# A Mamba layer and a mixture of experts on one core: long expert blocks of two sizes, and the seldom needed blocks behind four branches

## The chip, the cores and the metric

The kernel runs on one core of one Trainium2 chip. The metric is device time in microseconds (us); the time before is the median of three runs. Engines are named as in the profile: PE is the matrix engine (PEld its weight loads), DVE the vector engine, ACT the scalar engine, POOL the engine that issues indirect DMAs, SP the engine that issues plain DMAs. A "q" after a name (PEldq, DVEq) is that engine's instruction sequencer.

## The reference

The input is 4096 tokens of 256 numbers. A Mamba layer is added to it and normalised; every token of the result then goes through one of eight experts, and that is added and normalised again. All is float32. The experts are what the change touches:

```python
logits = xf @ Wr.T + br
expert_idx = jnp.argmax(logits, axis=-1)                 # one of 8 for each token
h = relu(einsum('td,efd->etf', xf, W1) + b1[:, None, :])  # 256 -> 1024
y = einsum('etf,efd->etd', h, W2) + b2[:, None, :]        # 1024 -> 256
x = layernorm(x + y[expert_idx, arange(T)])
```

With the inputs that are given, the reference's own arithmetic sends 495, 560, 487, 548, 514, 589, 514 and 389 tokens to the eight experts. In blocks of 128 that leaves 111, 48, 103, 36, 2, 77, 2 and 5 tokens over, and needs 37 blocks.

## The kernel before

The tokens go through Mamba in eight tiles of 512 (project, gauge, scan, gate, project_out). After each tile, choose, rank and place write each token's number into a list that is ordered by expert. The experts then work on blocks of up to 128 tokens of one expert: block b gathers its rows of x1 by an indirect DMA (L461), gathers its expert's weights into one of three buffers, b % 3 (L478), computes, and scatters its rows to the output by another indirect DMA (L589). Which expert and which rows a block has is known on the chip alone, so the number of blocks that the program holds is fixed: 32 that always run (SURE) and 7 more, of 39 in the worst case, that run only when they are needed.

A table tells each block its expert and its rows. Tables for the first 17 blocks are made early, when 3, 5 and 6 tiles are known; the last one (blocks_of, table, lookup) makes blocks 17 to 38 by a chain of small DVE instructions at 291 to 300 us, while blocks 8 and 9 run.

**Long blocks.** Five of the 32 blocks (LONG: 17, 20, 23, 26 and 29) are longer: they take 64 further rows of their expert, so that an expert with up to 64 tokens over needs no block for them. Given the counts above, five experts have 64 or fewer over, and 37 - 5 = 32 blocks are needed. A long block multiplies 192 columns at a time instead of 128 in its first layer (hidden, L526). In its second layer (close) the first 128 rows are done as in any block (pe, L551) and the further rows apart (pf, L562): their 64 columns take half of TensorE's columns, so two of the eight partial products run side by side, into two halves of one PSUM bank, and finish adds the two halves (L584).

**Order of a block.** The blocks function is a generator that yields after each quarter of a block: hidden(b, 0), hidden(b, 1), close(b, 0), close(b, 1). The transposes of the next block's rows (turn, L500 and L502) are put between hidden(b, 1) and close(b, 0). ACT evicts the first half of the hidden layer (L535), DVE the second (L537). After close, finish adds the residual (L573, L575) and normalises: DVE L252, L254 and L256, a square root on ACT (L257), DVE L258 and L259. PE's order is the order of the program; that of the other engines is made by the framework, which keeps what is inside a branch together and in its place. TensorE's results live in eight PSUM banks that one pool hands out in turn: three with the tag mm for hidden (two for an ordinary block, four for a long one), three with the tag o for pe and pf, two with the tag tr for the transposes.

**The branch.** Ahead of block 30 (BRANCH), seldom() gathers the rows of all seven blocks and opens one If on the number of blocks needed (held, read into a register of each engine while block 27 runs); all seven blocks stand in it, their weights loaded by SP. When it is not taken, each engine runs a short other side, which waits for the engine's own work and adds to its semaphore what the seven blocks would have added, and then jumps over the seven blocks. Block 30 is not turned ahead of the branch (`b + 1 not in (BRANCH, SURE)`), but after it.

Of the kernel before, what the change touches and what calls it, by code (L numbers as in the profile page):

```python
# [37 lines left out]
F32 = mybir.dt.float32  # L38
# [9 lines left out]
P = 128  # L48
# [25 lines left out]

EXTRA, MORE = 5, 64
LONG = {EARLY[6] + SLOTS * n: n for n in range(EXTRA)}
assert EXTRA <= RUN


BRANCH = SURE - 2  # L80
EPS = 1e-5
# [17 lines left out]
def mamba_moe(  # L99
# [179 lines left out]
    def table(b0, nb, columns, rows, early):  # L279
# [24 lines left out]
        if longer:  # L304

            low = small("low", [NE], I32)
            nc.vector.tensor_scalar(low, pn[:, 0:NE], float(MORE - 1), None, ALU.add)
            nc.vector.tensor_scalar(low, low, -P, None, ALU.bitwise_and)
            more = small("more", [NE])
            nc.vector.tensor_tensor(more, up, low, ALU.subtract)  # L310
            nth = small("nth", [NE])
            nc.vector.tensor_tensor(nth, low, taken, ALU.is_gt)
            nc.vector.tensor_tensor(more, more, nth, ALU.mult)

            nc.vector.tensor_tensor_scan(nth, ones8, more, 0.0, ALU.mult, ALU.add)
            nc.vector.scalar_tensor_tensor(
                more, nth, float(longer * P), more, ALU.is_le, ALU.mult
            )
            nc.vector.tensor_tensor(nth, nth, more, ALU.subtract)
            base = small("base", [1])  # L320
            nc.vector.tensor_reduce(base, more, AX.X, ALU.add)
            nc.vector.scalar_tensor_tensor(whole, more, -2.0, whole, ALU.mult, ALU.add)

            key = small("key", [NE])
            nc.vector.tensor_scalar(key, more, 0.0, float(OFF), ALU.is_equal, ALU.mult)
            nc.vector.tensor_tensor(key, key, nth, ALU.add)
            mine = small("mine", [longer, NE])
            nc.vector.tensor_tensor(mine, wide(key, longer), number(longer), ALU.is_equal)
            whose = small("whose", [longer, NE])
            nc.vector.tensor_tensor(whose, mine, wide(expertno, longer), ALU.mult)  # L330
            expert_of = small("expert_of", [longer])
            nc.vector.tensor_reduce(expert_of, whose, AX.X, ALU.add)
            nc.vector.tensor_scalar(key, low, -float(P + OFF), None, ALU.add)
            nc.vector.tensor_tensor(key, key, nth, ALU.subtract)
            nc.vector.tensor_tensor(mine, mine, wide(key, longer), ALU.mult)
            row_of = small("row_of", [longer])
            nc.vector.tensor_reduce(row_of, mine, AX.X, ALU.add)
        ends = small("ends", [NE])
        nc.vector.tensor_tensor_scan(ends, ones8, whole, 0.0, ALU.mult, ALU.add)
        if longer:  # L340
            nc.vector.tensor_scalar(ends, ends, base, None, ALU.add)
        starts = small("starts", [NE])
        nc.vector.tensor_tensor(starts, ends, whole, ALU.subtract)
        if not early:
            total = const.tile([1, 1], I32, name="total")
            nc.vector.tensor_copy(total, ends[0:1, NE - 1 : NE])
            held.append(total)
        shift = small("shift", [NE])
        nc.vector.scalar_tensor_tensor(shift, taken, -float(OFF), starts, ALU.add, ALU.subtract)


# [8 lines left out]
        if longer:  # L360
            nc.vector.tensor_tensor(row[:, 0:longer], row[:, 0:longer], row_of, ALU.add)
            nc.vector.scalar_tensor_tensor(
                row[:, nb:], row_of, float(P), blockoff[:, 0:longer], ALU.add, ALU.add
            )
# [10 lines left out]
        if not early:  # L375

            nc.vector.tensor_scalar(
                spare, eb[0:1, SURE - b0 : NSB - b0], float((NE - 1) * P), None, ALU.min
            )


            same = small("same", [nb])
            nc.vector.tensor_tensor(same[:, 1:nb], eb[:, 1:nb], eb[:, 0 : nb - 1], ALU.is_equal)
            nc.vector.memset(same[:, 0:nb:RUN], 0.0)
            nc.vector.scalar_tensor_tensor(eb, same, float(NE * P), eb, ALU.mult, ALU.add)
        widx = const.tile([P, nb], I32, name=f"widx{b0}")
# [10 lines left out]
        def lookup():  # L397

            pi = bank("tr", f"pi{b0}", 2)
            n = nb + longer  # L400
            for h in range(LH):
                nc.tensor.matmul(
                    pi[:, 0:n], lhsT=lists[:, h * P : (h + 1) * P], rhs=pick[:, h, :],
                    start=(h == 0), stop=(h == LH - 1),
                )
            codes = small("codes", [n])
            nc.scalar.copy(codes, pi[:, 0:n])
            half = small("half", [n])
            nc.vector.tensor_scalar(half, codes, 0.0, -float(T + 1), ALU.is_gt, ALU.mult)
            tidx = const.tile([P, n], I32, name=f"tidx{b0}")  # L410
            nc.vector.scalar_tensor_tensor(tidx, codes, float(T), half, ALU.add, ALU.add)
            for b in range(nb):
                index[b0 + b] = rows, tidx[:, order(b0, b)]
            for b, x in LONG.items() if longer else ():
                further[b] = tidx[0:MORE, nb + x : nb + x + 1]

# [39 lines left out]

    xgf, openf, yf, ends_, wide_ = {}, {}, {}, {}, {}
    current = 0
# [7 lines left out]
    def prefetch(b):  # L466
        for n in range(b, min(b + AHEAD, SURE - 1) + 1):
            if n in index and n not in xgs:
                xgs[n] = m3.tile([P, D], F32, tag="xg", name=f"xg{n}", bufs=4)
                gather(xgs[n], *index[n])  # L470
                if n in LONG:
                    ends_[n] = a2.tile([P, CC, KC - 1 + TB], F32, tag="xc", name=f"long{n}")
                    ends_[n] = ends_[n].rearrange("p c t -> p (c t)")
                    xgf[n] = ends_[n][0:MORE, 0:D]
                    gather(xgf[n], index[n][0], further[n])
# [7 lines left out]

    def rows_of(b):
        return P + MORE if b in LONG else P

    def buffer(b):
# [4 lines left out]
        return wide_[b]  # L492

    def turn(b):

        n = rows_of(b)
        px = bank("tr", f"pg{b}", 2)
        for dc in range(DC):
            at = slice(dc * P, (dc + 1) * P)
            nc.tensor.transpose(px[:, dc * n : dc * n + P], xgs[b][:, at], ident)  # L500
            if b in LONG:
                nc.tensor.transpose(  # L502
                    px[:, dc * n + P : (dc + 1) * n], xgf[b][:, at], ident[0:MORE, 0:MORE]
                )
        if b in LONG or b >= SURE:
            turned[b] = buffer(b)[:, FC * n : (FC + DC) * n]
        else:
            turned[b] = m2.tile([P, DC * P], F32, tag="xgT", name=f"xgT{b}")
        nc.vector.tensor_copy(turned[b], px[:, 0 : DC * n])

    def hidden(b, half):
        we, xgT, w = wes[b], turned[b], rows_of(b)
        if half == 0:
# [27 lines left out]
    def close(b, half):  # L541
# [15 lines left out]
        if b in LONG:  # L557

            openf[b] = bank("o", f"pf{b}")
            for fc in range(FC):  # L560
                g = fc % 2 * MORE
                nc.tensor.matmul(  # L562
                    openf[b][g : g + MORE, 0:D], lhsT=hT[:, fc, P:], rhs=out_weights(fc),
                    start=(fc < 2), stop=(fc >= FC - 2), tile_position=(0, g),
                )
        finish(b)

    def finish(b):
# [10 lines left out]
        if b in LONG:  # L579
            xs, r, yf[b] = (ends_[b][0:MORE, n * D : (n + 1) * D] for n in (1, 2, 3))  # L580
            nc.vector.tensor_tensor(xs, xgf[b], we[0:MORE, OC : OC + D], ALU.add)
            for g in range(2):
                part_sum = openf[b][g * MORE : (g + 1) * MORE, 0:D]
                nc.vector.tensor_tensor(r, part_sum, r if g else xs, ALU.add)  # L584
            layernorm(m2, r, yf[b], f"f{b}")
# [10 lines left out]

    def seldom():

        rows = a3.tile([P, CC, TB], F32, tag="cv", name="rows").rearrange("p c t -> p (c t)")
        for b in range(SURE, NSB):  # L600
            xgs[b] = ys[b] = rows[:, (b - SURE) * D : (b - SURE + 1) * D]
            gather(xgs[b], *index[b])
        with tc.If(held[1] > (SURE - EARLY[6]) * P, preferred_fallthrough_block=False):
            for b in range(SURE, NSB):
                wes[b] = held_weights[(BRANCH - 1) % SLOTS]
                row = nc.values_load(
# [10 lines left out]
    def blocks():  # L617

        nonlocal current
        for b in range(SURE):  # L620
            current = b
            if b == BRANCH:
                seldom()
            prefetch(b)

            if 0 < b:
                scatter(b - 1)
            if b == BRANCH:
                for n in range(SURE, NSB):
                    scatter(n)  # L630
            if b not in turned:
# [4 lines left out]
            yield  # L636
            if b + 1 in xgs and b + 1 not in (BRANCH, SURE):
                turn(b + 1)
# [432 lines left out]
    for _ in quarters:  # L1071
        if current == BRANCH - 3 and len(held) == 1:
            held += nc.values_load_multi_w_load_instructions(
                held[0], min_val=0, max_val=NSB * P, bass_reorder=False
            )[1]
    scatter(SURE - 1)

# [43 lines left out]
```

## Time and profile before

| what | us |
|---|---|
| median of three runs (502.12 to 507.25) | 503.51 |
| the profiled execution's own time | 497.31 |
| its span, first to last instruction | 495.3 |
| PE busy | 478.5 |
| DVE busy | 343.8 |
| from block 17's first L526 matmul to that of block 30 | 351.21 to 472.47 |
| table of blocks 17 to 38 on DVE (L297 to L387) | 291.6 to 299.3 |
| last matmul ends | 488.95 |

All expert blocks of the profile are the 32 that always run: L526 has 864 records of 128 columns, 27 blocks of 32, and 160 of 192 columns, 5 blocks of 32 (a float32 matmul shows as two records). The times are positions in the span, so that a row can be found in the timeline. A busy time of PE is the time in which at least one matmul is in flight.

### The profile page before, as it was taken

The page shows a single profiled execution, that of the slowest core. Times are in us where ns is not written, and L with a number is a line of the kernel's source. Part 1 is how long each engine was busy: PE and PEld are TensorE (multiplying, and loading weights), DVE is VectorE, ACT ScalarE, POOL GpSimd, SP SyncE. Part 2 cuts the span into 40 slices and gives each one's busy share as a digit, 9 for nine tenths or more (in the row PEclk, how much of TensorE's full clock was granted, in tenths as well). Part 3 has the DMA queues.
Part 4 walks back from the last instruction along what each step waited for, and adds up shares of the span by engine and source line. Part 5 has one row for each costly group of instructions (what it writes and reads, how often), then busy time and mean ns, then how long its engine had stood idle before and what let it go on. Part 6 is the DMA issues. An engine that isn't in the chain of part 4 may idle for free. (4 is left out here: it accounts for less than half of the span.)

```text
span 495.3 us, 7570 instructions
## 1 busy us (share of the span) xinstructions
PE 478.5 (97%) x2602; PEld 357.9 (72%) x2602; DVE 343.8 (69%) x1133; ACT 218.6 (44%) x452; POOL 187.2 (38%) x193
## 2 busy tenths in 40 slices
PE   8999999999999999999999999999999999999784
PEld 5444645555464676777889998999989898889684
DVE  2587979797999889869889786454454545455523
ACT  3786778787878774845351221122112121111101
POOL 2002122434456445223416133454444346373261
PEclk9999999999999999999999999999999999999979
DMA  7401012120309907507657597999861588479000
GB/s 233 155 1 44 0 44 85 44 85 9 120 1 370 340 23 266 192 0 259 223 222 256 201 349 288 353 330 354 340 256 47 194 286 244 172 239 387 25 4 22
DMA packets 23052, 87.46 MB, mean 177 GB/s; under 512 B 5026, under 2 KB 14757, under 8 KB 19426
## 3 DMA queue, kind: packets, MB, share of 16 engines
q0 software_dynamic: 8672, 72.15, 40.1%
q1 hardware_dynamic: 13378, 14.50, 9.0%
q8 instruction: 23, 0.38, 0.3%
q10 hardware_dynamic: 960, 0.27, 0.3%
q14 instruction: 19, 0.16, 0.1%
HBM read 87.45 MB, written 9.63 MB: 196 GB/s over the span
## 5 line engine op out<-in xcount | busy, mean ns | idle before, releaser
L667 PE MATMUL pm<-xTb,win 128*128 128x512 f32 (+1 forms) x260 | 120.9, 596 | 0.7 <-DMA xTb<-in_xT 0.7
L526 PEld LDWEIGHTS ph<-xgT,we 128*128 128x128 f32 x864 | 102.6, 195 | 6.7 <-issue 2.1
L526 PE MATMUL ph<-xgT,we 128*128 128x128 f32 x864 | 105.0, 279 | 0.9 <-issue 0.6
L551 PE MATMUL pe<-we,hT 128*128 128x256 f32 x432 | 100.1, 382 | 0.5 <-DVE hT L537 0.5
L551 PEld LDWEIGHTS pe<-we,hT 128*128 128x128 f32 x432 | 79.4, 190 | 12.0 <-DVE hT L537 1.7
L680 DVE SCALAR_TENSOR_TENSOR acc<-xc,cw,acc 128x512 f32<-128x512 f32 x96 | 71.2, 770 | 16.0 <-ACT acc L676 15.6
L667 PEld LDWEIGHTS pm<-xTb,win 128*128 128x128 f32 x260 | 47.4, 191 | 47.2 <-issue 40.7
L257 ACT ACTIVATE sdm<-sdm 128x1 f32<-128x1 f32 x32 | 6.5, 203 | 151.9 <-DVE sdm L256 151.8
L478 POOL DMA_INDIRECT we<-in_experts,widx x32 | 33.8, 1058 | 89.2 <-DVE r L575 50.4
L835 PE MATMUL po<-wout,sg 128*128 128x264 f32 x256 | 64.1, 392 | 0.1
L799 POOL TENSOR_TENSOR sg<-cv,sg 128x512 f32<-128x512 f32 x22 | 33.9, 1544 | 59.2 <-DVE cv L794 44.1
L835 PEld LDWEIGHTS po<-wout,sg 128*128 128x128 f32 x256 | 46.0, 190 | 10.2 <-issue 3.0
L589 POOL DMA_INDIRECT out<-y,tidx x32 | 32.9, 1028 | 53.0 <-DVE y L259 34.4
L535 ACT ACTIVATE hT<-ph,we 128x128 f32<-128x128 f32 x108 | 31.2, 366 | 34.0 <-PE ph L526 24.0
L537 DVE TENSOR_SCALAR hT<-ph,we 128x128 f32<-128x128 f32 x108 | 31.2, 341 | 21.2 <-PE ph L526 21.1
L575 DVE TENSOR_TENSOR r<-pe,xs 128x256 f32<-128x256 f32 x32 | 13.5, 422 | 45.4 <-PE pe L551 45.1
L461 POOL DMA_INDIRECT xg<-x1d,tidx x32 | 32.1, 1003 | 32.1 <-DVE xs L573 6.6
L924 POOL TENSOR_SCALAR rowh<-lrow,row,code 128x256 f16<-128x256 bf16 x20 | 25.8, 1297 | 26.7 <-DVE row L916 26.7
L794 DVE SCALAR_TENSOR_TENSOR cv<-cv,dp,py 128x256 f32<-128x256 f32 x64 | 28.9, 469 | 2.4 <-PE py L787 2.4
L526 PE MATMUL ph<-wide,we 128*128 128x192 f32 x160 | 26.8, 326 | 0.0
L672 ACT ACTIVATE sg<-pm 128x512 f32<-128x512 f32 x32 | 19.1, 596 | 17.1 <-PE pm L667 14.8
L526 PEld LDWEIGHTS ph<-wide,we 128*128 128x128 f32 x160 | 26.3, 190 | 0.3
(202 smaller groups left out, 611.2 us busy)
## 6 DMA issues: line engine op xcount, KB each, us to landing
xb<-in_x SPq DMA_DIRECT2D x8, 512.0 KB, 5.2
x1d<-x SPq DMA_DIRECT2D x8, 512.0 KB, 4.8
xTb<-in_xT SPq DMA_DIRECT2D x7, 512.0 KB, 3.3
win<-in_W_in SPq DMA_DIRECT2D x1, 512.0 KB, 5.8
we<-in_W_outT SPq DMA_DIRECT2D x1, 512.0 KB, 4.0
wout<-in_W_out SPq DMA_DIRECT2D x1, 512.0 KB, 4.9
we<-in_experts,widx POOLq DMA_INDIRECT x32, 9.7
xg<-x1d,tidx POOLq DMA_INDIRECT x32, 5.1
```

Source lines behind the costliest of these rows:

```text
L461: nc.gpsimd.indirect_dma_start(out=to, out_offset=None, in_=x1d[0:rows, :], in_offset=bass.IndirectOffsetOnAxis(ap=at, axis=0),)
L478: nc.gpsimd.indirect_dma_start(out=wes[n][:, :], out_offset=None, in_=experts, in_offset=bass.IndirectOffsetOnAxis(ap=weights[n], axis=0), ...
L526: nc.tensor.matmul(ph[:, n * w : (n + 1) * w], lhsT=we[:, at : at + P], rhs=xgT[:, dc * w : (dc + 1) * w], start=(dc == 0), stop=(dc == DC ...
L535: nc.scalar.activation(hT[:, fc, :], ph[:, n * w : (n + 1) * w], AF.Relu, bias=bias)
L537: last[b] = nc.vector.tensor_scalar(hT[:, fc, :], ph[:, n * w : (n + 1) * w], bias, 0.0, ALU.add, ALU.max)
L551: nc.tensor.matmul(py[:, 0:D], lhsT=hT[:, fc, 0:P], rhs=out_weights(fc), start=(fc == 0), stop=(fc == FC - 1),)
L589: moved = nc.gpsimd.indirect_dma_start(out=out, out_offset=bass.IndirectOffsetOnAxis(ap=at, axis=0), in_=rows, in_offset=None, bounds_chec ...
L667: nc.tensor.matmul(pm[:, at], lhsT=win[:, dc, c * P : (c + 1) * P], rhs=xTb[:, dc, at], start=(dc == 0), stop=(dc == DC - 1),)
L680: nc.vector.scalar_tensor_tensor(acc, xc[:, c, k : k + TB], cw[:, c, k : k + 1], acc, ALU.mult, ALU.add)
L794: nc.vector.scalar_tensor_tensor(cv[:, c, at], cv[:, c, at], dp[:, c : c + 1], py[:, 0 : TB // 2], ALU.mult, ALU.add,)
L799: eng.tensor_tensor(sg[:, c, :], cv[:, c, :], sg[:, c, :], ALU.mult)
L835: nc.tensor.matmul(po[:, 0 : D + NE], lhsT=sg[:, c, j * P : (j + 1) * P], rhs=wout[:, c, :], start=(c == 0), stop=(c == CC - 1),)
```

## The change

1. The five long blocks get two sizes (ROOM): 17, 20 and 23 take 32 further rows, 26 and 29 still 64. A block with 32 multiplies 160 columns in hidden. Its pf product takes a quarter of TensorE's columns, so that four partial products stand side by side, and finish adds four quarters instead of two halves.
2. The table sorts the experts: those with up to 32 over (few) get blocks 17, 20 and 23, those with 33 to 64 (more) get 26 and 29. This takes 22 more small DVE instructions.
3. The one branch becomes four: after block 27 (blocks 32 and 33), after 28 (34 and 35), after 29 (36) and after 31 (37 and 38). Block b + 1 is turned ahead of the branch, as in any block. The last branch stands ahead of finish(31). The register is read at block 24 instead of 27.
4. The seldom blocks' rows are gathered at blocks 22, 23, 24 and 26, and scattered at blocks 29, 30, 31 and the end, instead of all of them around block 30.
5. As the blocks behind the first two branches may overwrite a weight buffer, blocks 30 and 31 always load their weights, also where the block before in their buffer had the same expert.

```diff
-EXTRA, MORE = 5, 64
+ROOM = (32, 32, 32, 64, 64)
+EXTRA, LESS, MORE = len(ROOM), min(ROOM), max(ROOM)
-BRANCH = SURE - 2
+SELDOM = {SURE - 5: (0, 1), SURE - 4: (2, 3), SURE - 3: (4,), SURE - 1: (5, 6)}
...
+            for b in SELDOM:
+                if b + SLOTS < SURE:
+                    nc.vector.memset(same[:, order(b0, b + SLOTS - b0)], 0.0)
...
-    def rows_of(b):
-        return P + MORE if b in LONG else P
+    def more_of(b):
+        return ROOM[LONG[b]] if b in LONG else 0
...
+    def seldom_rows():
+        if not seldom_in:
+            rows = a3.tile([P, CC, TB], F32, tag="cv", name="seldom")
+            seldom_in.append(rows.rearrange("p c t -> p (c t)"))
+        return seldom_in[0]
+    def gather_seldom(b):
+        xgs[b] = ys[b] = seldom_rows()[:, (b - SURE) * D : (b - SURE + 1) * D]
+        gather(xgs[b], *index[b])
...
-            openf[b] = bank("o", f"pf{b}")
+            openf[b], n = bank("o", f"pf{b}"), more_of(b)
             for fc in range(FC):
-                g = fc % 2 * MORE
+                g = fc * n % P
                 nc.tensor.matmul(
-                    openf[b][g : g + MORE, 0:D], lhsT=hT[:, fc, P:], rhs=out_weights(fc),
-                    start=(fc < 2), stop=(fc >= FC - 2), tile_position=(0, g),
+                    openf[b][g : g + n, 0:D], lhsT=hT[:, fc, P:], rhs=out_weights(fc),
+                    start=(fc < P // n), stop=(fc >= FC - P // n), tile_position=(0, g),
                 )
-        finish(b)
+        if b != SURE - 1:
+            finish(b)
...
-            for g in range(2):
-                part_sum = openf[b][g * MORE : (g + 1) * MORE, 0:D]
-                nc.vector.tensor_tensor(r, part_sum, r if g else xs, ALU.add)
+            for g in range(0, P, m):
+                nc.vector.tensor_tensor(r, openf[b][g : g + m, 0:D], r if g else xs, ALU.add)
...
+    def seldom(after):
+        first = SURE + SELDOM[after][0]
+        with tc.If(held[1] > (first - EARLY[6]) * P, preferred_fallthrough_block=False):
+            for b in (SURE + n for n in SELDOM[after]):
+                wes[b] = held_weights[(after if after < SURE - 1 else after - 1) % SLOTS]
...
-            if b == BRANCH:
-                seldom()
+            if b - 1 in SELDOM:
+                seldom(b - 1)
             prefetch(b)
+            for n in SELDOM.get(b + 5, ()):
+                gather_seldom(SURE + n)
             if 0 < b:
                 scatter(b - 1)
-            if b == BRANCH:
-                for n in range(SURE, NSB):
-                    scatter(n)
+            for n in SELDOM.get(b - 2, ()):
+                scatter(SURE + n)
...
-            if b + 1 in xgs and b + 1 not in (BRANCH, SURE):
+            if b + 1 in xgs and b + 1 < SURE:
                 turn(b + 1)
...
-        if current == BRANCH - 3 and len(held) == 1:
+        if current == min(SELDOM) - 3 and len(held) == 1:
...
+    seldom(SURE - 1)
+    for n in SELDOM[SURE - 1]:
+        scatter(SURE + n)
+    finish(SURE - 1)
     scatter(SURE - 1)
```

## The prediction

> **What bounds the kernel.** I read the page's busy shares first, then who waited for whom, then PE's timeline from 445 us on, then the view of the branch's own line, L603.
>
> ```profile
> PE 478.5 (97%) x2602; PEld 357.9 (72%) x2602; DVE 343.8 (69%) x1133; ACT 218.6 (44%) x452; POOL 187.2 (38%) x193
> PEclk9999999999999999999999999999999999999979
> q8 instruction: 23, 0.38, 0.3%
> ```
>
> PE is the bound: 478.5 of 495.3 us. What PE saves in a block comes off the end if nothing else is late; what PE idles is added. The clock row has one dent, in the slice from 470 us.
>
> ```profile
> PE pg L500 <- DVEq L603: 3.8, 1, 3.8
> PE ph L526 <- issue: 0.6, 1, 0.6
> PE pe L551 <- DVE hT L537: 0.5, 1, 0.5
> ```
>
> These are all of PE's waits from 340 us on: four fifths stand at the branch.
>
> ```profile
> 448.72 3.73 PE L526 MATMUL ph<-xgT,we 128*128 128x128 f32 x32
> ...
> 456.72 5.36 PE L526 MATMUL ph<-wide,we 128*128 128x192 f32 x32
> 461.92 3.62 PE L551 MATMUL pe<-we,wide 128*128 128x256 f32 x16
> 465.47 1.95 PE L562 MATMUL pf<-we,wide 128*64 128x256 f32 x16
> 471.25 0.66 PE L500 MATMUL pg<-ident,xg 128*128 128x128 f32 x2 [3.83 <-DVEq L603]
> 472.47 5.78 PE L526 MATMUL ph<-xgT,we 128*128 128x128 f32 x32 [0.56 <-issue]
> 478.09 0.38 PE L500 MATMUL pg<-ident,xg 128*128 128x128 f32 x2
> 478.31 3.62 PE L551 MATMUL pe<-we,hT 128*128 128x256 f32 x16
> 481.76 3.73 PE L526 MATMUL ph<-xgT,we 128*128 128x128 f32 x32
> ```
>
> Block 29 ends at 467.42 and block 30's matmuls start at 472.47; the same 32 then take 5.78 us instead of 3.73.
>
> ```profile
> L603 PEldq COMPARE_BRANCH  x2: 95/1781/3467, 465.5 to 467.6; - x2
> L603 DVEq COMPARE_BRANCH  x2: 51/53/55, 469.8 to 470.7; - x2
> L603 DVEq EVENT_SEMAPHORE  x1: 21/21/21, 470.3 to 470.3; - x1
> ```
>
> The waits blame DVE, whose semaphore came at 470.3. But PE's second branch instruction, the jump over the seven blocks, starts at 467.6 and takes 3.467 us, to 471.1: PE was in its own jump. Every other engine's jump takes 0.04 to 0.06 us. Had the jump been quick, the transposes would still have waited for DVE until 470.3.
>
> [...] 0.38 MB in 23 packets of the instruction queue is 16 KiB each, and PE's long jump (7 blocks of about 100 records) stalls while short ones don't. [...] The trace shows half clock from 469.6 to 476.4, 6.83 us [...]
>
> **1. Removed: the stall at 467.** 5.05 us from 467.42 to 472.47, plus 5.78 - 3.73 = 2.05 us of half clock, less 0.22 us for which two transposes delay an ordinary block (478.09 to 478.31): -6.9 us.
>
> **2. Three narrower long blocks.** From the timeline, 32 first-layer records take 3.73 us at 128 columns and 5.36 at 192. 160 columns are not in the trace; halfway is 4.55, so -0.8 each (bounds 0 and -1.6). pf: 16 records of 64 columns take 1.95 us, two per 0.216 us. Quarters are in the trace in the router product L808 at 32 columns and the same 256 wide: 8 records in 0.64 us, four per 0.24 us or less. 16 of them take 4 x 0.216 + 0.24 = 1.1 us: -0.85 each (bounds 0, if the loads of the quarters queue, and -0.98). Together 3 x 1.65 = -5.0 us. Weights don't hold this back: each block's load is issued about two blocks ahead and lands in 9.7 us (page, DMA issues), and two ordinary blocks last 14.6.
>
> DVE gets 2 more adds (L584, 0.43 us each) per such block, 0.87 us, and pf ends 0.85 us earlier, so that DVE reaches the next block's evictions (L537) with about no reserve left: after block 26 it idled 0.66 us there, and PE needed them 1.2 us after they were done. I take +0.1 us per block, 0.3 in all; bounds 0 and 1.5.
>
> **3. Three branches in PE's way (27, 28, 29).** Two blocks are about 200 records and one 100[...]: I take 0.1 us for the jump, as PE's first branch (95 ns). But PE must first let its last matmul end and bump its semaphore: last matmul start + 0.38, semaphore and branch 0.3, restart 0.15, less the ordinary 0.22 between starts: +0.6 us.
>
> Then the wait behind it. The three mm banks are handed out in turn. Behind the branch after 27 come four uses (blocks 32, 33) and then block 28's first: its bank was last used by block 32's second half, which DVE evicts. On the path not taken, that count arrives when DVE itself passes the branch, after finish(27), which is ahead of it in DVE's queue. Same at 28. Finish is in the trace:
>
> ```profile
> 481.96 0.42 DVE L575 TENSOR_TENSOR r<-pe,xs 128x256 f32<-128x256 f32 x1 [1.83 <-PE pe L551]
> ...
> 483.73 0.41 DVE L259 TENSOR_SCALAR y<-r,mvm,sdm 128x256 f32<-128x256 f32 x1
> ```
>
> From the end of pe (478.31 + 3.62 = 481.93) to the end of y (484.14) is 2.21 us; with 0.2 for semaphore and restart PE idles 2.4, and as the next block usually starts 0.17 before pe ends (481.76), the loss is 2.6 us: twice, +5.2. After 29 only one block stands behind the branch (two banks), so block 30's first bank was freed by block 29 itself; its second needs ACT past the branch, which is there after 2.2 us, when PE comes: +0.6. Queued behind these waits: POOL's weights for 30 and 31 (issued some 2 us later, needed two blocks later: hidden) and ACT's first relu of 28 and 29 (PE isn't there earlier either).
>
> **4. Half clock.** [...] 2 x 1.1 = +2.2 us (bounds 0 and 3.4).
>
> **5. The table.** 22 more DVE instructions of about 0.15 us (L307 to L337 take 0.13 to 0.23), some 2 to 3.3 us, while DVE has no gap from 288 to 301. The next users: PE's list product L402 at 302.9 (the last pick is done at 298.5) and block 10's evictions from 303.1, ahead of which DVE idles 1.0 us. +0.3 (0 to 1.5).
>
> **6. Nothing added.** Gathers, scatters and the register read move to POOL and to queues ahead of their users; POOL is 38% busy. The forced weight loads of 30 and 31 are at most two of 9.7 us, issued two blocks (over 16 us) ahead; without that cover each would cost up to 9.7. The last branch: DVE reaches it when block 31's evictions end (486.7), 2 us before pe ends; its jump (0.5 us) and the scatters of 37 and 38 (1.3 us each on POOL) fit before y31 at 491.2. finish(31) stays 2.2 us.
>
> **Sum.** 497.31 - 6.9 - 5.0 + 0.3 + 5.2 + 0.6 + 2.2 + 0.3 = 494.0 us for the profiled execution, -3.3 us or a factor 0.9933. The median of the runs shown is 1.2% above that execution; 503.51 x 0.9933 = 500.2 us. The forecast's own range, with clock and DVE parts from none to their bounds, is 497 to 503.
>
> **Rivals.**
> - *PE doesn't wait for DVE after 27 and 28* (banks handed out otherwise, or finish behind the branch). Then each branch costs 0.6 and no clock: 497.31 - 11.9 + 1.8 + 0.6 = 487.8; 493.9 by the factor. For it: only the order of the banks says that PE waits. Against: in the trace the transposes did wait for DVEq L603. 12%.
> - *The gain of the narrow blocks is lost* (quarters queue, or DVE paces PE): up to 5 us less, 498.6; 504.8. For it: DVE's thin reserve. Against: L808. 15%.
> - *The jumps miss* (the other sign). [...] it costs 3.47 instead of 0.1: the loss is 0.6 + 3.4 = 4.0 us at each branch in place of 2.6, 2.6 and 0.6, so +6.2, [...] 503.1, or 509.4. Slower from two misses of three on. For it: four jumps in place of one. Against: other engines' jumps over up to 100 instructions don't stall. 13%.
> - The change does what it says: 32 blocks suffice, as three experts have at most 32 over and two 33 to 64, so no branch is taken.
>
> **How the numbers follow.** Forecast 60%. A difference of under 1% (5 us) can hardly be told from none here. Faster by more: 0.15 from the forecast's fast end and 0.12 from the first rival, 0.27. Slower by more: 0.12, the misses. Within 1%: 0.61. The range 493.5 to 506 takes in the first two rivals and leaves out the misses and the tails.
>
> **What would show it.** Right: L603's PE branches all near 0.1 us; PE waits of 2.4 us at ph L526 after blocks 27 and 28, put down to DVEq L603, and about 0.5 after 29; the clock's dents there; 128x160 records at 137 ns apart; pf of quarters in 1.1 us. Wrong: a PE branch of 3 us; no wait for DVE; PE waits for weights; or matmul groups of blocks 32 to 38, which would mean a branch was taken.

## The result and the profile after

| | median us | range | ratio to before, 95% interval |
|---|---|---|---|
| before, beside after | 503.47 | 502.12 to 507.25 | |
| after | 494.04 | 493.23 to 498.75 | 0.984, 0.980 to 0.988 |
| profiled execution of before, its span | 497.31, 495.31 | | |
| profiled execution of after, its span | 493.76, 492.06 | | |

The forecast for the profiled execution was -3.3 us, and it is -3.55 (the spans differ by 3.25). Of the medians it was also -3.3, and it is -9.4: 494.04 us, where 500.2 was forecast, in its own range 497 to 503. So the working can be followed term by term in the two traces, and what has to be explained besides is why the medians lie so much further apart than the traces.

The page of after: TensorE's busy time, and the clock in 40 slices.

```profile
PE 472.7 (96%) x2602; PEld 353.0 (72%) x2602; DVE 346.9 (71%) x1161; ACT 218.8 (44%) x452; POOL 187.3 (38%) x193
PEclk9999999999999999999999999999999999998997
```

TensorE is busy 5.8 us less for the same 2602 records, most of it in the three narrower blocks. Only one clock dent is left that isn't the end of the kernel, in slice 37 (443 to 455 us).

All waits of PE from 340 us on in after:

```profile
PE ph L581 <- DMA out<-long,tidx: 2.3, 1, 2.3
PE ph L581 <- DVEq L656: 2.3, 1, 2.3
PE pe L606 <- DVE hT L592: 0.7, 2, 0.4
PE ph L581 <- DVE y L261: 0.6, 1, 0.6
```

The 3.8 us at the transposes is gone. In its place stand two waits of 2.3 us and one of 0.6. The first names a DMA as its releaser; the timeline shows that it is the same wait as the second, one block earlier. PE's timeline, three windows of it:

```profile
399.37 4.51 PE L581 MATMUL ph<-wide,we 128*128 128x160 f32 x32
...
407.49 1.07 PE L617 MATMUL pf<-we,wide 128*32 128x256 f32 x16
...
445.16 5.47 PE L581 MATMUL ph<-xgT,we 128*128 128x128 f32 x32 [2.33 <-DMA out<-long,tidx]
...
457.38 0.92 PE L581 MATMUL ph<-wide,we 128*128 128x192 f32 x4 [2.32 <-DVEq L656]
...
469.04 3.81 PE L581 MATMUL ph<-xgT,we 128*128 128x128 f32 x32 [0.65 <-DVE y L261]
```

Block 23 now takes 4.51 us for 160 columns and 1.07 us for pf in quarters (5.36 and 1.95 before). Behind the branches PE idles 2.33, 2.32 and 0.65 us, and block 28's matmuls, at half clock from 445.70 to 449.11 us, take 5.47 us instead of 3.73. The branch's own line in after:

```profile
L656 PEldq COMPARE_BRANCH  x8: 64/190/310, 441.0 to 484.4; - x8
L656 DVEq COMPARE_BRANCH  x8: 43/48/55, 444.6 to 482.0; - x8
```

Each branch has two such instructions. PE's second, the jump over the blocks, takes 0.28 to 0.31 us at all four; none takes 3.47.

The same by stages. A stage runs from the first ph matmul of one block to that of another, in us; before_again and after_again are second executions of the two kernels, four_branches and split_finish are explained below.

| stage | before | before_again | four_branches | after | after_again | split_finish |
|---|---|---|---|---|---|---|
| start to 17 | 351.21 | 352.86 | 352.60 | 350.57 | 351.76 | 352.52 |
| 17 to 24 | 63.23 | 63.22 | 63.22 | 57.92 | 57.92 | 57.92 |
| 24 to 27 | 26.94 | 27.67 | 26.19 | 26.83 | 26.53 | 26.18 |
| 27 to 28 | 7.34 | 8.80 | 10.63 | 9.84 | 9.83 | 8.27 |
| 28 to 29 | 8.00 | 7.99 | 10.59 | 12.22 | 10.59 | 8.96 |
| 29 to 31 | 25.04 | 26.69 | 18.99 | 19.60 | 19.51 | 19.03 |
| 31 to end | 13.55 | 13.53 | 13.76 | 15.08 | 15.10 | 15.10 |
| span | 495.31 | 500.76 | 495.98 | 492.06 | 491.24 | 487.98 |

### The profile page after: what moved, and what is told of

It is laid out like the page before. It is cut to its first block, busy times and chain, and to the rows that moved or that the text cites. A ratio compares the mean times of both kernels' runs of the same rounds, so it can differ in the third digit from the quotient of the medians.

```text
span 492.1 us, 7641 instructions
## 1 busy us (share of the span) xinstructions
PE 472.7 (96%) x2602; PEld 353.0 (72%) x2602; DVE 346.9 (71%) x1161; ACT 218.8 (44%) x452; POOL 187.3 (38%) x193
## 5 line engine op out<-in xcount | busy, mean ns | idle before, releaser
L581 PE MATMUL ph<-wide,we 128*128 128x160 f32 (+1 forms) x160 | 24.4, 310 | 2.3 <-DVEq L656 2.3
L581 PEld LDWEIGHTS ph<-wide,we 128*128 128x128 f32 x160 | 23.8, 190 | 2.9 <-DVEq L656 2.7
```

The lines of the kernel that those rows point to most:

```text
L581: nc.tensor.matmul(ph[:, n * w : (n + 1) * w], lhsT=we[:, at : at + P], rhs=xgT[:, dc * w : (dc + 1) * w], start=(dc == 0), stop=(dc == DC ...
```

## The experiments

They ran in three groups of four, each group on one chip: A (before there 502.33 us), B (499.24) and C (502.32). Ratios are to before on the same chip.

### Group A: the parts apart

**before_again and after_again** are the two kernels unchanged.

> The kernel before, unchanged, once more with a profile. Its first profiled execution took 497.31 us, but its other executions 502 to 507. If the extra 5 to 6 us are part of what the branch does ([...] the half clock lasts longer), this profile shows over 8 us lost between the end of block 29 and block 31 instead of 6.9, and the stages before are as they were (block 17 starts at 351 us). If they come from elsewhere, block 17 starts 5 us later, or a stage between has a wait that the first profile had not, and the branch still costs 6.9. If it is chance, this profile lies at 497 again.

> The changed kernel, unchanged, once more. In its first profile the last scatter started 1.8 us after its rows were ready (488.2 against 486.4), where before it took 0.3. If that is part of the change it is there again; if chance, the scatter starts within 0.4 us. PE's gaps after 27, 28 and 29 are 2.3, 2.3 and 0.65 us again; the clock halves after none, one or both of the first two.

Measured: before_again 502.10 us, ratio 0.999 (0.997 to 1.001); after_again 495.76, ratio 0.989 (0.985 to 0.992). The trace of before_again (502.77) is 5.5 us longer than the first one of before, and the table shows where: 1.46 us between 27 and 28, 0.73 between 24 and 27 (block 24 takes 1.48 us more, block 25 0.74 less, since the first trace had a smaller delay there), 1.65 from 29 to 31, 1.65 before block 17. From 29 to 31 nearly all of it is in block 30, behind the jump: 30 to 31 takes 10.86 us instead of 9.29. So the first trace of before was of a quick execution: its 497.31 us is below every run of before on chips A and C (500.09 at least), though not below all those on chip B (496.23 to 502.83). Which chip it ran on is not on record.

**four_branches** (label four_branches_only): the change without the two sizes.

```diff
-ROOM = (32, 32, 32, 64, 64)
+ROOM = (64, 64, 64, 64, 64)
```

> The four branches alone: all five long blocks have 64 further rows again. If the parts add up, block 24 starts 5.2 us later than in the changed kernel, the idle times of PE after blocks 27, 28 and 29 stay 2.3, 2.3 and 0.65 us, and this kernel is 5 us slower than the changed one: about 499 us for an execution like the profiled one of before (497.3), that is no gain against it. Rival: if the medians' difference of 9.4 us comes from the branches for the most part, this kernel is about 5 us faster than before in the timed rounds.

Measured: 500.32 us, ratio 0.996 (0.994 to 0.998). The gaps behind the branches are 3.12, 2.32 and 0.65 us, with no half clock. The first is 0.8 us longer than expected; why, no run shows. So the branches and gathers alone bring 2.0 us on this chip, and the two sizes the other 4.6 (500.32 to 495.76).

**two_sizes_one_branch**: the change with all seven blocks behind one branch, after block 29. All seven rows are scattered at block 30, as in before, and no branch stands at the end.

```diff
-SELDOM = {SURE - 5: (0, 1), SURE - 4: (2, 3), SURE - 3: (4,), SURE - 1: (5, 6)}
+SELDOM = {SURE - 3: (0, 1, 2, 3, 4, 5, 6)}
```

> The two sizes of long blocks, with one branch after block 29 that holds all seven seldom blocks (block 30 is turned ahead of it). My theory[...]: PE's jump over some 700 records takes 3.4 us as before, PE idles 3.9 us there and the clock halves; the three narrow blocks save 5.2 us, so this is about 5 to 6 us under the kernel before. Rival, that PE's stall was DVE's lateness: the idle time falls to 0.7 us because block 30 is turned ahead, and this is about 11 us under.

Measured: 507.34 us, ratio 1.011 (1.006 to 1.016). The branch's line and PE's timeline of this kernel:

```profile
L656 PEldq COMPARE_BRANCH  x2: 95/1810/3526, 471.2 to 473.3; - x2
```

```profile
430.04 6.10 PE L606 MATMUL pe<-we,hT 128*128 128x256 f32 x16 [5.29 <-ACT hT L590]
...
476.97 2.05 PE L581 MATMUL ph<-xgT,we 128*128 128x128 f32 x8 [3.89 <-DVEq L656]
480.46 5.28 PE L581 MATMUL ph<-xgT,we 128*128 128x128 f32 x24 [1.44 <-issue]
```

The jump over seven blocks takes 3.526 us again, though block 30 was turned ahead of it; PE idles 3.89 us, its next matmuls run at half clock and it waits 1.44 us more without a releaser in the trace. The instruction queue (q8) moves one packet of 16 KiB inside this jump, from 474.30 to 475.44 us, and the next from 477.46 to 478.94, just ahead of that last wait. In before such a packet starts at 468.63 us, 1.0 us into the jump; in after none starts inside the four jumps over one or two blocks. So a packet goes with the far jump; what the jump waits for, no run shows. Turning block 30 early doesn't shorten it. But the jump isn't all of the stall: VectorE passed this branch at 475.9 us, 1 us before PE started again, so by this estimate a quick jump alone would have saved some 1 us of the 3.89. one_two_two_two, below, shows the rest. And there is something that nobody had forecast: the seven gathers, here in one bunch at 411 to 419 us, are followed by a stall at 420 to 430 us, in which block 25 takes 19.9 us and not 8. That gave a new theory: **gathers of the seldom blocks in a bunch hold up the engines.** In before they stand one, three and three together, and the two bunches of three lie just ahead of the two places where before_again lost 1.5 us.

### Group B: the waits and the gathers

**split_finish**: the residual sum and layernorm of 27 and 28 behind the branch; add makes the sum of rows and bias alone, in a buffer of its own.

```diff
-        if b != SURE - 1:
+        if b in (SURE - 5, SURE - 4):
+            add(b, "xsd")
+        elif b != SURE - 1:
             finish(b)
...
                 seldom(b - 1)
+                if b - 1 in (SURE - 5, SURE - 4):
+                    finish(b - 1)
```

> The kernel after, with the residual sum and the layernorm of blocks 27 and 28 moved behind the branch that follows them; only the sum of rows and bias stays ahead of it, so VectorE reaches both branches before TensorE does. Theory: TensorE's two gaps of 2.32 us are its wait for VectorE, which has to finish the block before it may jump; they fall to about 0.65 us, the gap after block 29 stays at 0.65, no window is at half clock, and the time falls by about 3.3 us against the kernel after (to 491 to 493 us). Rival: the gaps are the jumps themselves, or the work that was put off now holds up the next block; the gaps stay over 2 us or come back further on, and the time is 494 to 497 us.

Measured: 490.85 us (489.80 to 492.65), ratio 0.984 (0.981 to 0.987). PE's waits from 340 us on, and its timeline at the two branches:

```profile
PE ph L581 <- DVE r L640: 1.5, 2, 0.8
PE ph L581 <- DVE long L649: 0.7, 1, 0.7
```

```profile
444.89 3.81 PE L581 MATMUL ph<-xgT,we 128*128 128x128 f32 x32 [0.75 <-DVE r L640]
...
453.85 0.40 PE L581 MATMUL ph<-wide,we 128*128 128x192 f32 x1 [0.73 <-DVE r L640]
```

With VectorE past the branch first, the gaps fall from 2.33 and 2.32 to 0.75 and 0.73 us, and no half clock follows them (the clock is 1.00 from 405 to 455 us). The wait was for VectorE behind finish, as forecast. Its span is 3.3 us shorter than that of after_again, on another chip; 3.2 of it lies in the two stages behind these branches.

**one_two_two_two**: the seven blocks divided 1, 2, 2, 2.

```diff
-SELDOM = {SURE - 5: (0, 1), SURE - 4: (2, 3), SURE - 3: (4,), SURE - 1: (5, 6)}
+SELDOM = {SURE - 5: (0,), SURE - 4: (1, 2), SURE - 3: (3, 4), SURE - 1: (5, 6)}
```

> The kernel after, with the seven seldom blocks divided 1, 2, 2, 2 over the four branches in place of 2, 2, 1, 2. Theory: whether TensorE waits for VectorE behind a branch is set by the bank that its next matmul gets, and two banks per seldom block in a rotation of three decide it: with one block in the branch the bank was drained before, with two it is the one that VectorE frees last. So the gaps become 0.65 us after block 27, 2.3 us after 28 and about 3 us after 29 (a long block, whose end takes VectorE longer); together 0.6 us more than after, time 494 to 497 us. Rival: place decides, not the bank: 2.3, 2.3 and 0.65 us as in the kernel after.

Measured: 496.12 us, ratio 0.994 (0.991 to 0.996); gaps 0.65 after 27, 2.32 after 28, 3.09 after 29. Its waits of PE, and PE behind the branch after 29:

```profile
PE ph L581 <- DVEq L656: 5.4, 2, 3.1
PE ph L581 <- DVE r L631: 0.6, 1, 0.6
```

```profile
470.78 5.47 PE L581 MATMUL ph<-xgT,we 128*128 128x128 f32 x32 [3.09 <-DVEq L656]
```

The short gap moved from the branch after 29 to that after 27, with the single block. So the number of blocks in the branch decides which branch waits, not the place, and the rival falls. That is what the rotation of the banks foretold; the number of banks itself was not varied. This run also shows what made the stall from 29 to 31 go: its jump after 29 takes 0.311 us, and still 29 to 31 takes 24.62 us, against 25.04 in before and 18.99 in four_branches. Of the 5.63 us to four_branches, 2.44 are the longer gap (3.09 instead of 0.65) and about 3.2 two stretches of half clock, one behind the gap after 28 and one behind this gap. So the short jump is needed, but most of the gain comes from PE's not having to wait for VectorE there.

**before_gathers_spread**: before, with the seven gathers apart (the framework issued them as 1, 1, 2, 1 and 2).

```diff
+            for n in {22: (0, 1), 23: (2, 3), 24: (4,), 26: (5, 6)}.get(b, ()):
+                gather_seldom(SURE + n)
...
-            gather(xgs[b], *index[b])
```

> The kernel before, with one edit: the gathers of the seven seldom needed blocks, whose 128 descriptors each read one and the same spare row here, stand apart in blocks 22, 23, 24 and 26 in place of one, three and three together. Theory: such gathers in a bunch of three hold the DMA engines and stop TensorE for 1.2 us twice (1.21 us at 420.1 and 1.18 us at 447.8 in the second profile of before); apart, both gaps fall under 0.4 us and the time falls by 2 to 3 us, to about 500 us, ratio 0.995. Rival: the bunches cost nothing as a rule, since the first profile of before had hardly a gap there; ratio 1.000.

Measured: 498.37 us, ratio 0.998 (0.9965 to 1.0001). In its trace the two stalls are absent: 24 to 25 takes 7.35 us and 27 to 28 7.35. But the time is at most 1.8 us less than before's, perhaps not less at all, and before itself is 3 us quicker on chip B than on A. The forecast of 2 to 3 us was missed here. There is no trace of before on chip B, so the missing stalls can't be put down to the edit.

**rows_inside**: gathers and scatters of the seldom blocks inside the branches.

```diff
             for b in (SURE + n for n in SELDOM[after]):
+                gather_seldom(b)
...
+                scatter(b)
...
-            for n in SELDOM.get(b + 5, ()):
-                gather_seldom(SURE + n)
...
-            for n in SELDOM.get(b - 2, ()):
-                scatter(SURE + n)
```

> The kernel after, with the gathers and scatters of the seven seldom blocks inside the branches, so that none of the fourteen is made here. Theory: the two gaps of 0.35 to 0.39 us that the gathers leave go, and the last scatter no longer stands 1.8 us behind its block, if the two scatters ahead of it are the cause: 0.8 to 2.6 us less than after, 492 to 494 us. Rival: POOL now has to take the branches too, so the weight loads queued behind it wait for its jumps and for its own outstanding work, and TensorE waits for weights or rows in blocks 30 and 31: 495 us or more.

Measured: 500.17 us, ratio 1.001 (0.999 to 1.004). The last scatter does follow its block at once (0.28 us), no gap of 0.35 us is left (nor is there one in split_finish, which kept the gathers), and no block waits for weights or rows. But POOL's drain at the end of the program takes 9.94 us where split_finish has 3.02, and that moves the end by 6.9 us. What it waits for the trace doesn't show. Both the expected gain and the expected loss were off.

### Group C: what is it about the gathers?

**before_third** is before, unchanged. **before_own_rows** lets each empty place of a block gather a spare row of its own, where all of them read one row; **one_branch_own_rows** is two_sizes_one_branch with the same edit.

```diff
-    x1d = dram.tile([T + 1, D], F32, name="x1d")
+    x1d = dram.tile([T + P, D], F32, name="x1d")
...
+            if not early:
+                own = small("own", [n])
+                nc.vector.tensor_scalar(own, codes, 0.0, part[:, 0:1], ALU.is_equal, ALU.mult)
+                nc.vector.tensor_tensor(half, half, own, ALU.add)
```

> The kernel before, unchanged, for its trace beside the next three on one chip. If the gathers in bunches of three cost time, it shows gaps of about 1.2 us near blocks 24 and 27 as the second profile of before did (both blocks 8.8 us in place of 7.35); if those were chance, both blocks take 7.3 to 7.5 us. Time 499 to 503.5 us.

> The kernel before, with as many gathers in the same bunches, but with 128 spare rows in place of one: each empty place of a block gathers a row of its own. Theory: what holds the DMA engines is that 128 descriptors read the same row, not their number; no gap at blocks 24 and 27 is left and the time is 1 to 3 us less than before. Rival: the bunch of three is too much work for the queue whatever it reads; as before, ratio 1.000.

> The earlier kernel with the two sizes and one branch after block 29, whose seven gathers stand together, with the same 128 spare rows. Theory of the same row: the stall of some 12 us at blocks 24 and 25 goes, block 25 takes 7.3 to 8.5 us and not 19.9, and the time is about 495 us, 0.985 to 0.99 of before. Rival, the number of descriptors: the stall stays, 505 us or more. In both cases TensorE's jump after block 29 still costs 3.4 to 4 us, since the seven blocks that it jumps over are as long as in the kernel before.

Measured: before_third 503.31 us, ratio 1.001 (0.999 to 1.003); before_own_rows 502.99, ratio 1.001 (1.000 to 1.003); one_branch_own_rows 509.45, ratio 1.014 (1.012 to 1.016). before_third has both stalls (8.81 and 8.81 us), before_own_rows too (8.74 and 8.79), and in one_branch_own_rows block 25 takes 19.7 us. So the theory of the one row falls. For the bunch of seven, what counts is the bunch, whatever it reads: on chip A after (as after_again) and two_sizes_one_branch differ only in how the seven blocks are divided over branches, and with it their gathers, and only the second has the stall. For the bunches of three it isn't shown, as before and the spread gathers didn't run on one chip.

The one row does show in the DMA engines. The same 3 us inside the long stall, in two_sizes_one_branch and then in one_branch_own_rows; the last three numbers are PE's clock, the DMA engines' busy share and GB/s:

```profile
423.00:426.00 3.00, 0.48 (x2) 0.14 (x1) 0.00 (x0) 0.00 (x0) 2.26 (x3) 0.78 1.02 81
```

```profile
423.00:426.00 3.00, 0.48 (x2) 0.27 (x2) 0.40 (x1) 0.00 (x0) 2.39 (x3) 0.98 0.23 73
```

With one row the DMA engines are busy all the time and move little: the packets of 4096 bytes take 0.76 us (median from 417 to 428 us). With a row for each place they take 0.17 us (419 to 430) and the engines are mostly idle, but block 25 takes 19.7 us and not 19.9. So busy DMA engines are not what stops the others. How the shorter stall looks, first PE and then ACT in before_third, then ACT in before_gathers_spread at the same block:

```profile
416.92 3.84 PE L526 MATMUL ph<-xgT,we 128*128 128x128 f32 x32
...
422.17 3.72 PE L551 MATMUL pe<-we,hT 128*128 128x256 f32 x16 [1.20 <-ACT hT L535]
```

```profile
421.75 0.37 ACT L535 ACTIVATE hT<-ph,we 128x128 f32<-128x128 f32 x1 [5.08 <-PE pg L500]
```

```profile
418.50 0.37 ACT L535 ACTIVATE hT<-ph,we 128x128 f32<-128x128 f32 x1 [2.38 <-DMA xg<-x1d,tidx]
```

With the gathers spread, ACT's first relu of block 24 starts 2.1 us after PE's first matmul (416.36); with the bunch, 4.8 us after it, though PE went through its matmuls at its usual pace and the weights had landed. The releaser that the first ACT line names, the transposes, is not what the relu needs. So an engine stood still without a reason that the trace gives.

**split_own_rows**: split_finish and the spare rows together.

> The kernel after with the two layernorms behind their branches (the edit of split_finish) and the 128 spare rows as well. If the gathers from one row still cost something when they stand apart: 0.3 to 0.8 us less than split_finish's ratio of 0.984, about 0.982 of before; if not, the same ratio. In no case slower by over 0.5 us, as two short VectorE instructions on the way to the last table are all that is added.

Measured: 489.80 us (489.06 to 491.82), ratio 0.976 (0.973 to 0.978); gaps of 0.76, 0.73 and 0.65 us, no half clock. In time it lies 1.05 us below split_finish, on another chip, so the spare rows themselves aren't shown to bring anything. The ratio lies below both forms of the forecast (0.982 and 0.984), but ratios from two chips, with before 3 us apart, can't be compared so finely. With either form the edit of split_finish beats before on the same chip. after ran on neither of these chips, so what the edit brings against it is read from the stages: 3.2 us.

## Why the prediction was right, and where it was off

**1, the stall (-6.9, with +0.6 for the branch after 29): right.** From 29 to 31, 25.04 us became 19.60, where 18.74 was forecast; four_branches has 18.99. It took both things that the prediction named: the short jump (two_sizes_one_branch keeps the long one, and the stall) and a next bank that doesn't wait for VectorE (one_two_two_two has the short jump and still 24.62 us). In after, 0.35 of the rest is a wait for VectorE's hT in block 30.

**2, the narrow blocks (-5.0): right.** 17 to 24, which holds all three, is 5.31 us shorter. The +0.3 for VectorE's further adds isn't seen: block 24 starts without a wait. Its second half waits 0.39 us for VectorE in after and 0.2 in after_again, but not in split_finish, which has the same adds.

**3, the waits behind 27 and 28 (+2.6 each): right in size and cause.** 27 to 28 is 2.50 us longer, 28 to 29 2.59 (after_again, full clock). split_finish confirms VectorE's finish as what is waited for; one_two_two_two fits the banks. The jump is 0.28 to 0.31 us and not 0.1, the author's estimate; the wait for VectorE hides the difference except after 29.

**4, the half clock (+2.2): about right.** It was the author's estimate, as were the 2.9 us of half clock in the third rival (500.2 to 503.1 us); what lowers the clock isn't shown. One stretch of half clock in after, 445.70 to 449.11 us, costs 12.22 - 10.59 = 1.6 us; after_again has none. Of eight gaps of 2.3 to 3.1 us, three were followed by half clock: one of two in after (2.33, 2.32), none in after_again (2.3 twice) and four_branches (3.12, 2.32), both in one_two_two_two (2.32, 3.09). So the length of the gap alone doesn't decide it. In the traces of before and after the changes of the clock lie whole steps of 3.41 us apart (6.83 and 17.07 us in before, 3.41 and 37.55 in after). Counted in these steps, PE was idle for 2.16 us (before) and 2.33 us (after) in the step ahead of the fall, and for 0.89 and 1.44 us in the two steps that share after's second gap, where the clock stayed. That some gaps are followed by half clock and some not may also be why the runs of after differ: its six runs in group A have mean clocks of 0.986 to 0.995, and the two slowest in time (498.48 and 498.05) both have 0.986.

**5, the table (+0.3): not seen.** Start to 17 differs by 0.6 us in after's favour, less than the first three traces of before differ among themselves (351.21 to 353.69).

**6, "Nothing added": this step failed, twice.** First, the end. In before the scatter of block 31 starts 0.28 us after y31; in after, 1.82 us. POOL's timeline in after:

```profile
483.49 0.97 POOL L645 DMA_INDIRECT out<-seldom,tidx  x1 [0.30 <-issue]
488.20 0.98 POOL L645 DMA_INDIRECT out<-y,tidx  x1 [3.74 <-issue]
```

y31 was done at 486.38, and the two scatters of 37 and 38 were through at 484.46: they fit, as the prediction had it, and the scatter was late all the same, by 1.5 us more than before. after_again, one_two_two_two and split_finish have the same 1.8 us, two_sizes_one_branch too, without a branch at the end; four_branches (0.28) and rows_inside don't. four_branches differs from after in the sizes alone, so the delay comes with the two sizes, and rows_inside, which makes no seldom gather or scatter, shows that it takes those too. By which way, no run shows.

Second, the gathers. I asked only whether the moved gathers cost anything. That something was lost behind each bunch of three, 1.5 us in later traces of before, the first one hardly showed: it lost 0.74 us at block 25 and nothing after the second bunch.

**The sum** held for the traces because these misses cancel: +1.5 at the end and +0.9 from 29 to 31, against -0.6 before block 17, -0.6 at the clock, -0.3 each at the narrow blocks, VectorE's adds and the table, and -0.2 in smaller ones. No term of the forecast foresaw the +1.5, so that the sum came out to 0.1 us was luck.

**The median** failed in one place, the last factor: 503.51 x 0.9933. It took the 6.2 us between that trace and the median to be spread over the kernel, to stay whatever was changed. The second and third traces of before show what they are made of: 2.2 us more from 24 to 28, where the stalls are, which after hardly has, and 1.7 to 2.3 us more from 29 to 31 (26.69 and 27.38 us, 25.04 in the first). Of the latter the jump itself is only 0.1 to 0.3 us (3.542 and 3.806 us, 3.467 in the first); the rest is in block 30. What is left lies before block 17, where after_again is longer too. Taken off with -3.3, that gives some -7 to -8 as an estimate; group A measured -6.6, the first comparison -9.4 with an interval from -6 to -10. The change was most likely to stay within 1%, and brought 1.6% (1.2 to 2.0). That 494.04 us still lies in the wide range from 493.5 to 506 is luck: its lower edge was drawn for the first rival, PE without a wait for VectorE (493.9), and the traces show that wait.

**What stays open** is what stops the engines behind a bunch. One sign is in the recording: POOL's 120 DMAs leave 16 marks each as they land, 1920 in all (1915 are there in the first trace of before). The traces of before_again, before_third, before_own_rows, and of the two kernels with one bunch of seven, which all have the stall, hold 1127 to 1180 of them; those of chip B and the first of before, without it, all but 16 at most (rows_inside, with fewer DMAs, all but 9). Kernels without a bunch lack such marks too in the first comparison and on chips A and C (after 1236, four_branches 1327), so the loss isn't the stall, but the two go with the same chips. In the one full trace of before, the first, the bunches didn't stall PE by over a microsecond; and chip B is the one on which before is 3 us quicker, so that first trace may owe its quickness to its chip. Whether the stall depends on the chip, or on the recording itself, no run here shows: I didn't measure before's stalls on chip B, nor before with its gathers spread on A or C.

## What to carry to other kernels

A short jump is not enough: in one_two_two_two it takes 0.311 us, and PE idles 3.09 us. Before a branch, let the engine that others will wait for pass it early: put the work that it need not finish (here two layernorms, which cut PE's gaps from 2.33 and 2.32 to 0.75 and 0.73 us) behind the branch, and ask what the next buffer in rotation was last used by on the path not taken. When the one trace at hand is quicker than every run beside it, the difference may be a cost that this trace doesn't show, and just what the change removes; it is not to be scaled over the sum. Dummy work that "costs nothing because it is hidden" deserves a look at how it stands in its queue: on chip A seven gathers together cost 12 us where the same seven apart cost under one.

## What the runs showed of the hardware

- TensorE's jump over one or two blocks takes 0.28 to 0.31 us in after (up to 0.40 in split_finish), over seven 3.467 (before), 3.526 (two_sizes_one_branch) and 3.806 (before_third). A 16 KiB packet of the instruction queue starts 1.0 us into the long jump in before and in two_sizes_one_branch (468.63 and 474.30 us), and inside none of the four short ones in after.
- TensorE's clock was at one half for 6.83 us from 469.58, inside the gap of 3.83 us in before, and for 3.41 us from 445.70, behind one of 2.33 us in after; behind after's other gap, of 2.32 us, it stayed at full speed, and so it did behind 3.12 us in four_branches.
- Seven indirect gathers of 128 rows of 1 KB in one bunch were followed by a stall of about 12 us of PE, VectorE and ACT (block 25 took 19.9 us in two_sizes_one_branch and 19.7 in one_branch_own_rows, chips A and C), three by one of 1.5 us (before_again, before_third and before_own_rows, on the same chips; in the first trace of before by 0.74 us at most, and on chip B not traced).
- When all 128 places of such gathers read one row, packets of 4096 bytes took 0.76 us instead of 0.17 (two_sizes_one_branch, one_branch_own_rows); the stall was the same.
